# A fixed-point layer in half-batch units, with interval and remainder read from the bits of the shifted value

## The chip, the core and the metric

The kernel runs on one core of a Trainium2 chip. The core has five engines with a queue each: TensorE (PE, matrix products; PEld is its loading of weights), VectorE (DVE), ScalarE (ACT), GpSimd (POOL) and SyncE (SP, which only starts transfers here). Each engine works through its own queue in order; semaphores make an instruction wait for results of other engines. The metric is the device time of one execution in microseconds, lower is better.

## What is computed

The program is a decoder of four layers; each adds an attention, a cross attention and a feed-forward part to the token vectors `x` (8 batches of 256 tokens, 256 features) and normalises after each. The change concerns the very last part, the feed-forward of the fourth layer, a multilayer perceptron in fixed point with a piecewise-linear gelu:

```python
def float2fix(x, bits):                     # round to multiples of 2**-bits
    return round(x * 2**bits) / 2**bits
def pwlin_gelu_basic(x, bits_in, bits_out):
    xq = float2fix(x, bits_in)
    y = interp(xq, _PWL_X, _PWL_Y)          # gelu at 33 points, -4 to 4 in steps of 0.25
    y = where(xq > 4.0, xq, where(xq < -4.0, 0.0, y))
    return float2fix(y, bits_out)
h = einsum('bsd,df->bsf', x, w1) + b1       # 256 -> 1024
h = float2fix(h, 8)
h = pwlin_gelu_basic(h, 8, 8)
h = float2fix(h, 8)
out = einsum('bsf,fd->bsd', h, w2) + b2     # 1024 -> 256
return float2fix(out, 8)
...
x = _layernorm(x + _L3_ffn_ref(x, L3_ffn_w1, L3_ffn_b1, L3_ffn_w2, L3_ffn_b2), axis=-1)
```

In units of 1/256 a hidden value is an integer v; an interval of the gelu is 64 of these units. With n the interval of v (its floor division by 64) and r = v - 64n, the value is `256 gelu(n/4) + 4 (gelu((n+1)/4) - gelu(n/4)) r`, rounded.

## The kernel before

The tokens lie in SBUF twice: `X`, 16 tiles of 128 tokens by 256 features, and `xT`, its transpose, two blocks of 128 features by 2048 tokens. The last parts of the program run batch by batch (256 tokens, two tiles): `l2_ffn` interleaves by hand the expert part of the third layer with `convolve(b)` and `attend(b)`, the two attentions of the fourth layer, for the batch before. After its loop it still has the attentions of batch 7 to issue (`for _ in later: pass`), and then it calls `fixed_point`.

`fixed_point` loops over the 8 batches (`o` in steps of T = 256 tokens). One batch:

- eight blocks of hidden features, two to a PSUM tile `ph`: products with `w1` (L132, each written as two passes in the trace), and one ACT eviction per block with scale 256 and bias (L1594) into `v`, 128 x 2048;
- DVE rounds v by adding and subtracting ROUND = 1.5 x 2^23 (L1596), and finds the interval n in two operations (L1598, L1599);
- ACT takes the gelu at both ends of the interval, `low` (L1601) and `high` (L1603), 128 x 2048 each;
- DVE makes the remainder v - 64n (L1604), the difference high - low (L1605), the product with the remainder (L1606), adds 256 low (L1607) and rounds (L1608);
- for each of the two token tiles PE multiplies v by `w2` (L132, 16 passes) and adds the bias b2 with a product of ones and a row (L134); DVE rounds the result (L1615) and adds the residual (L1616);
- `finish` normalises: statistics on DVE (L163, L164), the inverse root on POOL (L141, L143, since `power` is set for this part), scaling into X on DVE (L187); SP stores each tile to the output.

The pools give `v`, `low`, `high`, `z`, `q` two buffers and `n` one; `ph` and `po` have two PSUM banks each.

The order of the instructions on each engine is not that of the text. When the program is built, a planner with its own estimates of durations takes from all instructions whose operands are ready the one that stands first in the text, engine by engine, and inserts the waits. So the attention of batch 7 comes first where it is ready, and `fixed_point` of the earlier batches fills what is left: on PE, products of its first batch stand at 2508.6 us, before the attention of batch 6 is done at 2551.

Of the kernel before, what the change touches and what calls it, by code (L numbers as in the profile page):

```python
# [11 lines left out]
F32 = mybir.dt.float32  # L12
BF16 = mybir.dt.bfloat16
I32 = mybir.dt.int32
U32 = mybir.dt.uint32
AF = mybir.ActivationFunctionType
ALU = mybir.AluOpType
# [3 lines left out]
P = 128  # L21
B, S, D = 8, 256, 256
NT = B * S // P
NTOK = B * S
# [3 lines left out]
ROUND = 1.5 * 2.0**23  # L28
# [14 lines left out]
class Net:  # L43
# [1241 lines left out]
    def l2_ffn(self, w):  # L1285


        tc = self.tc
        with ExitStack() as ctx:
            w3 = self.load(  # L1290
                ("l3a_win", 2), ("l3a_wout", 2), *((f"l3x_w{n}", 4 if n == "o" else 2) for n in "qkvo"),
                rows=("l3a_bout", "l3a_ln_w", "l3a_ln_b", "l3x_bo"),
            )
            win, wout, wq, wk, wv, wo, bout, ln_w, ln_b, bo = w3
            pool3 = ctx.enter_context(tc.tile_pool(name="a3", bufs=1))
            ps3 = ctx.enter_context(tc.tile_pool(name="a3p", bufs=2, space=PSUM))
            convolve = self.convolution_batches((win, wout, bout, ln_w, ln_b), pool3, ps3)
            attend = self.context_batches((wq, wk, wv, wo, bo), pool3, ps3)
            later = iter(())
            with (  # L1300
                tc.tile_pool(name="f2", bufs=1) as pool,
                tc.tile_pool(name="f2w", bufs=2) as work,
                tc.tile_pool(name="f2p", bufs=2, space=PSUM) as ps,
            ):
                experts = self.expert_batches(w, pool, work, ps)
                for b in range(B):
                    experts(b, later)
                    later = chain(convolve(b), attend(b))
            w4 = self.load(("l3f_w1", 2), ("l3f_w2", 8), rows=("l3f_b2",))
            pool = ctx.enter_context(tc.tile_pool(name="f3", bufs=1))  # L1310
            work = ctx.enter_context(tc.tile_pool(name="f3w", bufs=2))
            ps = ctx.enter_context(tc.tile_pool(name="f3p", bufs=2, space=PSUM))
            for _ in later:
                pass
            self.power = True
            self.fixed_point(w4, pool, work, ps)
# [256 lines left out]
    def fixed_point(self, w, pool, work, ps):  # L1573

        nc = self.nc
        w1, w2, b2_row = w
        FC, T = 8, 256
        ONE = 256.0  # L1580
        b1 = pool.tile([P, FC], F32, name="b1")
        nc.vector.tensor_scalar(b1, self.col("l3f_b1"), ONE, None, ALU.mult)
        b2 = pool.tile([1, D], F32, name="b2")
        nc.vector.tensor_scalar(b2, b2_row, ONE, None, ALU.mult)
        for o in range(0, NTOK, T):
            v = work.tile([P, FC, T], F32, name="v")
            for f in range(0, FC, 2):
                ph = ps.tile([P, 2, T], F32, name="ph")
                for m in range(2):
                    g = f + m  # L1590
                    self.mm(
                        ph[:, m, :], [(w1[:, c, g * P : (g + 1) * P], self.xT[:, c, o : o + T]) for c in range(2)]
                    )
                    nc.scalar.activation(v[:, g, :], ph[:, m, :], AF.Identity, bias=b1[:, g : g + 1], scale=ONE)  # L1594
            v = v.rearrange("p f t -> p (f t)")
            nc.vector.tensor_scalar(v, v, ROUND, ROUND, ALU.add, ALU.subtract)  # L1596
            n = work.tile([P, FC * T], F32, name="n", bufs=1)
            nc.vector.tensor_scalar(n, v, 1 / 64, -31.5 / 64, ALU.mult, ALU.add)  # L1598
            nc.vector.tensor_scalar(n, n, ROUND, ROUND, ALU.add, ALU.subtract)  # L1599
            low = work.tile([P, FC * T], F32, name="low")  # L1600
            nc.scalar.activation(low, n, AF.Gelu, scale=0.25)  # L1601
            high = work.tile([P, FC * T], F32, name="high")
            nc.scalar.activation(high, n, AF.Gelu, bias=self.cst("quarter"), scale=0.25)  # L1603
            nc.vector.scalar_tensor_tensor(v, n, -64.0, v, ALU.mult, ALU.add)  # L1604
            nc.vector.tensor_tensor(high, high, low, ALU.subtract)  # L1605
            nc.vector.scalar_tensor_tensor(v, high, 4.0, v, ALU.mult, ALU.mult)  # L1606
            nc.vector.scalar_tensor_tensor(v, low, ONE, v, ALU.mult, ALU.add)  # L1607
            nc.vector.tensor_scalar(v, v, ROUND, ROUND, ALU.add, ALU.subtract)  # L1608
            h = v.rearrange("p (f t) -> p f t", t=T)
            z = work.tile([P, 2, D], F32, name="z")  # L1610
            for j in range(2):
                po = ps.tile([P, D], F32, name="po")
                self.mm(po, [(h[:, f, j * P : (j + 1) * P], w2[:, f, :]) for f in range(FC)], bias=b2)
                q = work.tile([P, D], F32, name="q")
                nc.vector.tensor_scalar(q, po, ROUND, ROUND, ALU.add, ALU.subtract)  # L1615
                nc.vector.scalar_tensor_tensor(  # L1616
                    z[:, j], q, 1.0 / ONE, self.X[:, o // P + j, :], ALU.mult, ALU.add
                )
            self.finish(o // P, 1, z, self.last)

# [425 lines left out]
```

## Time and profile before

| what | us |
|---|---|
| three runs of the kernel before | 2783.50, 2792.79, 2794.55 |
| their median | 2792.79 |
| the profiled execution, its own time | 2775.67 |
| span of the profiled execution, first to last instruction | 2773.9 |
| first product of `fixed_point` on PE | 2508.6 |
| first L1596 on DVE | 2566.7 |
| last attention operation on DVE (L1565 of batch 7) | 2642.5 |
| last L1608 ends, the last products with `w2` begin | 2754.2 |

The mean TensorE clock granted over the span was 0.873. In a row of the profile "busy" is the time in which an engine had an instruction running; a row of instructions gives engine, operation, output and inputs by the program's names and their count. Lines of the trace can be merged: "x2" is two instructions one after the other. In the rows by stretch each engine's busy time is followed by its number of instructions, then come the granted clock of TensorE, the share of the transfer engines and GB/s. The list of waits reads "who <- whom: total us, times, longest".

### The profile page before, as it was taken

The numbers are of one execution on the slowest core, as the hardware profiler recorded it, in microseconds if no ns is written. First come the engines' busy times: TensorE is split into PE (matmuls) and PEld (weight loads), VectorE is DVE, ScalarE is ACT, GpSimd is POOL, SyncE is SP. The second block draws the span as 40 slices with busy tenths as digits, with TensorE's granted clock in tenths as the row PEclk, the third lists the DMA queues.
The fourth block names the chain that finished last, engine by engine and source line by source line (L and its number), as shares of the span: only waits on it lengthen the run. The fifth ranks groups of instructions, "written<-read, shape, count | busy, mean of one in ns | idle before, by whom it ended". The sixth has DMA issues, their size and how long they took to land.

```text
span 2773.9 us, 40937 instructions
## 1 busy us (share of the span) xinstructions
PE 2171.2 (78%) x14331; PEld 1571.3 (57%) x14331; DVE 1681.6 (61%) x5714; ACT 957.4 (35%) x2197; POOL 891.8 (32%) x949
## 2 busy tenths in 40 slices
PE   8978688699988788438975767887878868777975
PEld 5554588555565467415544345666756656555654
DVE  4654300266667575356767876758668666654876
ACT  2322133234333442104432333343534435433431
POOL 1020121221111124451110136666566565660000
PEclk9988699899998779759997878889989888887987
DMA  2001243200010137420010011111111111120000
GB/s 81 2 1 42 105 149 108 69 7 1 1 62 16 36 106 220 141 80 1 1 42 16 1 65 46 45 43 47 38 41 47 40 43 43 52 73 3 1 20 12
DMA packets 84173, 135.04 MB, mean 49 GB/s; under 512 B 33445, under 2 KB 53045, under 8 KB 82048
## 3 DMA queue, kind: packets, MB, share of 16 engines
q0 software_dynamic: 52288, 79.27, 9.7%
q1 hardware_dynamic: 28924, 49.45, 5.3%
q10 hardware_dynamic: 2756, 3.72, 0.4%
q8 instruction: 114, 1.87, 0.3%
q14 instruction: 91, 0.75, 0.1%
HBM read 242.90 MB, written 17.70 MB: 94 GB/s over the span
## 4 chain that ended last, share of the span: by engine, by line
PE 25%; DVE 16%; issue 6%; ACT 3%; another core or an unknown queue 2%; POOL 2%; DMA 0%; ACTq 0%; POOLq 0%; DVEq 0%
PE po L1401 5%; PE pp L132 4%; PE s L132 4%; PE po L132 3%; DVE junk L1349 2%; DVE low L478 1%; PE ph L132 1%; PE s L1547 1%; PE sc L132 1%; PE s L1525 1%; POOL rows L893 1%; PE po L1382 1%; PE sc L445 1%; DVE X L187 1%
## 5 line engine op out<-in xcount | busy, mean ns | idle before, releaser
L893 POOL DMA_INDIRECT rows<-in_l2f_table_dram,index x512 | 530.5, 1036 | 348.8 <-issue 110.7
L1401 PE MATMUL po<-rows,diag 128*128 128x256 f32 x768 | 231.2, 437 | 90.7 <-ACT diag L1400 54.4
L1349 DVE SCALAR_TENSOR_TENSOR junk<-rows,X 128x256 f32<-128x256 f32 x512 | 214.9, 420 | 53.6 <-DMA rows<-in_l2f_table_dram,index 28.4
L1401 PEld LDWEIGHTS po<-rows,diag 128*128 128x128 f32 x768 | 153.0, 213 | 142.8 <-ACT diag L1400 67.2
L132 PE MATMUL pp<-xT,w 128*128 128x256 f32 (+1 forms) x672 | 196.9, 435 | 35.1 <-issue 20.4
L132 PE MATMUL ph<-xeT,we 128*128 128x128 f32 x1248 | 183.7, 291 | 20.9 <-DMA we<-in_l0f_experts_dram,wrow 16.5
L132 PEld LDWEIGHTS ph<-xeT,we 128*128 128x128 f32 x1248 | 170.1, 201 | 41.7 <-DMA we<-in_l0f_experts_dram,wrow 17.9
L553 POOL TENSOR_TENSOR aT<-sides,inv 128x256 f32<-128x256 f32 x64 | 46.8, 731 | 441.6 <-DVE sides L551 275.3
L132 PEld LDWEIGHTS pp<-xT,w 128*128 128x128 f32 x672 | 141.6, 218 | 69.2 <-issue 29.7
L1400 ACT ACTIVATE diag<-ident,dots 128x128 f32<-128x128 f32 x384 | 134.1, 394 | 129.9 <-PE po L1401 58.8
L173 PE MATMUL pt<-ident,X 128*128 128x128 f32 x352 | 76.3, 330 | 117.6 <-DVE X L187 68.9
L174 ACT COPY xT<-pt 128x512 f32<-128x512 f32 x88 | 51.6, 587 | 328.1 <-PE pt L173 229.7
L893 POOL DMA_INDIRECT xe<-xd,take x87 | 85.2, 979 | 208.0 <-PE pt L908 81.6
L141 POOL TENSOR_SCALAR rs_v<-ln_mv 128x2 f32<-128x2 f32 x48 | 12.5, 260 | 389.8 <-DVE ln_mv L164 362.1
L173 PEld LDWEIGHTS pt<-ident,X 128*128 128x128 f32 x352 | 49.4, 163 | 152.7 <-issue 73.0
L132 PE MATMUL py<-we,hT 128*128 128x256 f32 x496 | 129.8, 386 | 0.9 <-DVE hT L1037 0.9
L1014 DVE TENSOR_TENSOR y<-py,we 128x256 f32<-128x256 f32 x23 | 9.8, 425 | 199.0 <-PE py L132 199.0
L517 ACT ACTIVATE e<-sc 128x512 f32<-128x512 f32 (+1 forms) x155 | 82.0, 602 | 107.2 <-PE sc L445 93.5
L1008 ACT ACTIVATE hT<-ph,we 128x128 f32<-128x128 f32 x184 | 65.5, 367 | 121.0 <-PE ph L132 91.3
L187 DVE TENSOR_SCALAR X<-z,ln_mv,rs_y 128x256 f32<-128x256 f32 x192 | 73.3, 424 | 54.3 <-POOL rs_y L143 52.4
L445 PE MATMUL sc<-kv,qv 32*128 32x128 f32 (+2 forms) x1448 | 99.8, 315 | 2.5 <-DVE sides L551 1.0
L445 PE MATMUL sc<-qv,kv 32*128 32x128 f32 (+2 forms) x1396 | 99.1, 347 | 0.0
(492 smaller groups left out, 5205.2 us busy)
## 6 DMA issues: line engine op xcount, KB each, us to landing
we<-in_l1f_experts_dram SPq DMA_DIRECT2D x32, 384.0 KB
yd<-y SPq DMA_DIRECT2D x32, 256.0 KB
rows<-in_l2f_table_dram,index POOLq DMA_INDIRECT x512
w<-in_l2x_w_dram SPq DMA_DIRECT2D x1, 4096.0 KB
yd<-y SPq DMA_DIRECT2D x23, 128.0 KB
X<-in_x_dram SPq DMA_DIRECT2D x8, 256.0 KB
xd<-X ACTq DMA_DIRECT2D x8, 256.0 KB
xd<-X SPq DMA_DIRECT2D x8, 256.0 KB
```

The source lines that it names most:

```text
L132: self.nc.tensor.matmul(out, lhsT=lhsT, rhs=rhs, start=n == 0, stop=n == last and bias is None)
L173: nc.tensor.transpose(pt[:, c, j, :], self.X[:, i0 + j * step, c * P : (c + 1) * P], self.ident)
L174: nc.scalar.copy(self.xT4[:, :, i0 : i0 + step + 1 : step, :], pt)
L187: nc.vector.tensor_scalar(self.X[:, i, :], z[:, j, :], mv[:, j, 0:1], r[:, j : j + 1], ALU.subtract, ALU.mult)
L445: nc.tensor.matmul(sc[: shape[0], part], lhsT=lhsT, rhs=rhs, start=mask is None, stop=True, skip_group_check=True)
L517: lambda r, sc: nc.scalar.activation(e0[m][:n0, r], sc, AF.Exp),
L553: nc.gpsimd.tensor_tensor(out, split(both), split(inv), ALU.mult)
L893: self.nc.gpsimd.indirect_dma_start(out=out, out_offset=None, in_=table, in_offset=bass.IndirectOffsetOnAxis(ap=index, axis=0), **({} if r ...
L1008: nc.scalar.activation(hT[:, g + f, :], ph[:, f, :], AF.Gelu, bias=b1[:, g + f : g + f + 1])
L1349: nc.vector.scalar_tensor_tensor(junk, row, 1.0, self.X[:, i, :], ALU.mult, ALU.mult, accum_out=out)
L1400: nc.scalar.activation(diag, self.ident, AF.Copy, scale=dots[:, k : k + 1])
L1401: nc.tensor.matmul(po, lhsT=diag, rhs=rows[:, k, D:], start=False, stop=g + k == H * K - 2)
```

## The change

A unit is now half of a batch's hidden features (four blocks, 128 x 1024), 16 units in all, and a loop issues for each u the steps `first(u + 2)`, `gelu(u + 1)`, `between(u)` and `second(u)`. `first` adds ROUND on ACT and leaves it in: the low bits of the float are then the integer v. `gelu` shifts these bits right by six and flips the exponent bits, which makes the float 2^23 + 2^16 + n, in one DVE operation; the gelus take the offset off again by their bias (a column of `shift`). A second DVE operation keeps the low six bits and sets an exponent so that the float is 2^25 + 4r. The difference of the gelus is formed by GpSimd. `between` has three DVE operations: remainder times difference, plus 256 low, rounding. `second` runs for every second unit: the products of both token tiles go into one PSUM bank, b2 is added by DVE from a tile that was spread over the partitions once at the start, and rounding and residual take both tiles at once. `v`, `n`, `q`, `z` have two buffers of half or double width, `low` and `high` three, `f` four.

```diff
@@ l2_ffn @@
-            work = ctx.enter_context(tc.tile_pool(name="f3w", bufs=2))
+            work = ctx.enter_context(tc.tile_pool(name="f3w", bufs=3))
@@ fixed_point @@
-        FC, T = 8, 256
+        FC, T, H = 8, 256, 4
...
-        b2 = pool.tile([1, D], F32, name="b2")
-        nc.vector.tensor_scalar(b2, b2_row, ONE, None, ALU.mult)
-        for o in range(0, NTOK, T):
-            v = work.tile([P, FC, T], F32, name="v")
...
-            v = v.rearrange("p f t -> p (f t)")
-            nc.vector.tensor_scalar(v, v, ROUND, ROUND, ALU.add, ALU.subtract)
-            n = work.tile([P, FC * T], F32, name="n", bufs=1)
-            nc.vector.tensor_scalar(n, v, 1 / 64, -31.5 / 64, ALU.mult, ALU.add)
-            nc.vector.tensor_scalar(n, n, ROUND, ROUND, ALU.add, ALU.subtract)
-            low = work.tile([P, FC * T], F32, name="low")
-            nc.scalar.activation(low, n, AF.Gelu, scale=0.25)
-            high = work.tile([P, FC * T], F32, name="high")
-            nc.scalar.activation(high, n, AF.Gelu, bias=self.cst("quarter"), scale=0.25)
-            nc.vector.scalar_tensor_tensor(v, n, -64.0, v, ALU.mult, ALU.add)
-            nc.vector.tensor_tensor(high, high, low, ALU.subtract)
-            nc.vector.scalar_tensor_tensor(v, high, 4.0, v, ALU.mult, ALU.mult)
-            nc.vector.scalar_tensor_tensor(v, low, ONE, v, ALU.mult, ALU.add)
-            nc.vector.tensor_scalar(v, v, ROUND, ROUND, ALU.add, ALU.subtract)
...
+        b2 = pool.tile([P, D], F32, name="b2")
+        pp = ps.tile([P, 2, T], F32, name="ph")
+        nc.tensor.matmul(pp[:, 0, :], lhsT=self.ones, rhs=b2_row, start=True, stop=True)
+        nc.scalar.mul(b2, pp[:, 0, :], ONE)
+        shift = pool.tile([P, 3], F32, name="shift")
+        for n, value in enumerate((ROUND, -0.25 * (2.0**23 + 2.0**16), -0.25 * (2.0**23 + 2.0**16 - 1.0))):
+            nc.gpsimd.memset(shift[:, n : n + 1], value)
+        units = [(o, h) for o in range(0, NTOK, T) for h in range(0, FC, H)]
+        vs, fs, gelus = {}, {}, {}
+
+        def first(u):
+            o, h = units[u]
+            v = vs[u] = work.tile([P, H, T], F32, name="v", bufs=2)
...
+                    nc.scalar.activation(v[:, f + m, :], ph[:, m, :], AF.Identity, bias=b1[:, g : g + 1], scale=ONE)
+            nc.scalar.activation(v, v, AF.Identity, bias=shift[:, 0:1])
+
+        def gelu(u):
+            v = vs.pop(u).rearrange("p f t -> p (f t)").bitcast(I32)
+            n = work.tile([P, H * T], F32, name="n", bufs=2)
+            nc.vector.tensor_scalar(
+                n.bitcast(I32), v, 6, 0x4B000000 ^ 0x4B000000 >> 6, ALU.arith_shift_right, ALU.bitwise_xor
+            )
+            low = work.tile([P, H * T], F32, name="low")
+            nc.scalar.activation(low, n, AF.Gelu, bias=shift[:, 1:2], scale=0.25)
+            high = work.tile([P, H * T], F32, name="high")
+            nc.scalar.activation(high, n, AF.Gelu, bias=shift[:, 2:3], scale=0.25)
+            f = fs[u] = work.tile([P, H * T], F32, name="f", bufs=4)
+            nc.vector.tensor_scalar(f.bitcast(I32), v, 63, 0x4C000000, ALU.bitwise_and, ALU.bitwise_or)
+            nc.gpsimd.tensor_tensor(high, high, low, ALU.subtract)
+            gelus[u] = low, high
+
+        def between(u):
+            low, rise = gelus.pop(u)
+            f = fs[u]
+            nc.vector.scalar_tensor_tensor(f, f, 2.0**25, rise, ALU.subtract, ALU.mult)
+            nc.vector.scalar_tensor_tensor(f, low, ONE, f, ALU.mult, ALU.add)
+            nc.vector.tensor_scalar(f, f, ROUND, ROUND, ALU.add, ALU.subtract)
+
+        def second(u):
+            o, h = units[u]
+            if h == 0:
+                return
...
             for j in range(2):
-                po = ps.tile([P, D], F32, name="po")
-                self.mm(po, [(h[:, f, j * P : (j + 1) * P], w2[:, f, :]) for f in range(FC)], bias=b2)
...
+                self.mm(
+                    po[:, j, :], [(fb[f // H][:, f % H, j * P : (j + 1) * P], w2[:, f, :]) for f in range(FC)]
                 )
+            q = work.tile([P, 2, D], F32, name="q", bufs=2)
+            nc.vector.tensor_tensor(q, po, b2.unsqueeze(1).to_broadcast([P, 2, D]), ALU.add)
+            nc.vector.tensor_scalar(q, q, ROUND, ROUND, ALU.add, ALU.subtract)
...
+        count = len(units)
+        for u in range(-2, count):
+            if u + 2 < count:
+                first(u + 2)
+            if 0 <= u + 1 < count:
+                gelu(u + 1)
+            if u >= 0:
+                between(u)
+                second(u)
```

More of the change, by code (lines that the diff above doesn't have):

```diff
@@ L1582, in fixed_point @@
         nc.vector.tensor_scalar(b1, self.col("l3f_b1"), ONE, None, ALU.mult)
-        b2 = pool.tile([1, D], F32, name="b2")
-        nc.vector.tensor_scalar(b2, b2_row, ONE, None, ALU.mult)
-        for o in range(0, NTOK, T):
-            v = work.tile([P, FC, T], F32, name="v")
-            for f in range(0, FC, 2):
+        b2 = pool.tile([P, D], F32, name="b2")
[10 more added lines that the diff above has]
+            v = vs[u] = work.tile([P, H, T], F32, name="v", bufs=2)
+            for f in range(0, H, 2):
                 ph = ps.tile([P, 2, T], F32, name="ph")
                 for m in range(2):
-                    g = f + m
+                    g = h + f + m
                     self.mm(
@@ L1593, in fixed_point @@
                     )
-                    nc.scalar.activation(v[:, g, :], ph[:, m, :], AF.Identity, bias=b1[:, g : g + 1], scale=ONE)
-            v = v.rearrange("p f t -> p (f t)")
-            nc.vector.tensor_scalar(v, v, ROUND, ROUND, ALU.add, ALU.subtract)
-            n = work.tile([P, FC * T], F32, name="n", bufs=1)
-            nc.vector.tensor_scalar(n, v, 1 / 64, -31.5 / 64, ALU.mult, ALU.add)
-            nc.vector.tensor_scalar(n, n, ROUND, ROUND, ALU.add, ALU.subtract)
-            low = work.tile([P, FC * T], F32, name="low")
@@ L1608, in fixed_point @@
-            nc.vector.tensor_scalar(v, v, ROUND, ROUND, ALU.add, ALU.subtract)
-            h = v.rearrange("p (f t) -> p f t", t=T)
-            z = work.tile([P, 2, D], F32, name="z")
-            for j in range(2):
-                po = ps.tile([P, D], F32, name="po")
-                self.mm(po, [(h[:, f, j * P : (j + 1) * P], w2[:, f, :]) for f in range(FC)], bias=b2)
[L1614 to L1617, printed above, removed]
-                )
@@ new lines, in between @@
+        def between(u):
[8 more added lines that the diff above has]
+                return
+            fb = [fs.pop(n).rearrange("p (f t) -> p f t", t=T) for n in (u - 1, u)]
+            po = ps.tile([P, 2, D], F32, name="po")
+            for j in range(2):
+                self.mm(
+                    po[:, j, :], [(fb[f // H][:, f % H, j * P : (j + 1) * P], w2[:, f, :]) for f in range(FC)]
+                )
+            q = work.tile([P, 2, D], F32, name="q", bufs=2)
+            nc.vector.tensor_tensor(q, po, b2.unsqueeze(1).to_broadcast([P, 2, D]), ALU.add)
+            nc.vector.tensor_scalar(q, q, ROUND, ROUND, ALU.add, ALU.subtract)
+            z = work.tile([P, 2, D], F32, name="z", bufs=2)
+            nc.vector.scalar_tensor_tensor(z, q, 1.0 / ONE, self.X[:, o // P : o // P + 2, :], ALU.mult, ALU.add)
+            self.finish(o // P, 1, z, self.last)
```

## The prediction

> **What bounds the kernel now.** First the page's head; then, since the changed function is the program's last stage, the busy table by stretch from 2551 us (the attention of token batch 6 ends there) to the end; then the chain of waits and the wait list there; last, two places where GpSimd and VectorE met.
>
> ```profile
> span 2773.9 us, 40937 instructions
> ...
> PE 2171.2 (78%) x14331; PEld 1571.3 (57%) x14331; DVE 1681.6 (61%) x5714; ACT 957.4 (35%) x2197; POOL 891.8 (32%) x949
> ```
>
> ```profile
> 2551.00:2577.00 26.00, 24.13 (x101) 17.95 (x102) 17.11 (x42) 16.41 (x28) 0.00 (x0) 0.88 0.00 0
> 2577.00:2620.00 43.00, 37.38 (x164) 28.71 (x163) 42.88 (x55) 15.93 (x22) 0.00 (x0) 0.92 0.00 1
> 2620.00:2647.00 27.00, 25.93 (x151) 21.09 (x149) 12.29 (x43) 11.79 (x30) 2.02 (x4) 1.00 0.00 1
> 2647.00:2691.00 44.00, 30.51 (x123) 23.15 (x124) 35.88 (x45) 14.34 (x17) 2.80 (x4) 0.84 0.07 24
> 2691.00:2735.00 44.00, 36.16 (x142) 28.18 (x141) 33.16 (x34) 16.43 (x24) 1.85 (x4) 0.88 0.04 12
> 2735.00:2774.00 39.00, 13.21 (x47) 9.34 (x45) 19.49 (x24) 4.28 (x3) 2.79 (x4) 0.71 0.04 13
> ```
>
> Columns after the length: PE, PEld, DVE, ACT, POOL busy, then the granted clock. DVE is full at first (42.88 of 43 us), PE is full while the attention of batch 7 runs, and from 2647 on neither is.
>
> ```profile
> 2745.98 2.30 DVE high L1605
> 2748.30 2.30 DVE v L1606
> 2750.63 2.30 DVE v L1607
> 2752.95 1.24 DVE v L1608
> 2754.24 5.76 PE po L132 x16
> ```
>
> ```profile
> PE po L132 <- DVE v L1608: 35.1, 4, 16.7
> ...
> ACT low L1601 <- DVE n L1599: 31.7, 6, 9.8
> ```
>
> The chain is that of the last batch: DVE alone from 2745.98, then PE, whose first 16 passes take 5.76 us (3.72 at full clock). PE waited 35.1 us in all for the last rounding, and the gelus 31.7 us for the interval, since whole batches go through DVE, ACT, DVE and PE in turn. L1605 starts at 2658.65, 2702.24 and 2745.98 for every second batch: 43.7 us for two, 21.8 us a batch.
>
> ```profile
> 1549.82 2.50 POOL L1815 TENSOR_TENSOR z<-X,b 128x512 f32<-128x512 f32 x2 [29.68 <-ACT b L1797]
> ...
> 1549.80 1.37 DVE L1790 SCALAR_TENSOR_TENSOR top<-top,cat_sc,bias 128x64 f32<-128x64 f32 x1
> 1551.21 1.17 DVE L1791 TENSOR_SCALAR top<-top 128x64 f32<-128x64 f32 x1
> ...
> 2650.87 1.16 POOL L141 TENSOR_SCALAR rs_v<-ln_mv 128x2 f32<-128x2 f32 x1 [3.96 <-DVE ln_mv L164]
> ...
> 2650.73 1.23 DVE L1598 TENSOR_SCALAR n<-v 128x2048 f32<-128x2048 f32 x1
> ```
>
> Two DVE operations on 64 columns took 1.37 and 1.17 us, each until a GpSimd addition was over; a GpSimd operation on two columns took 1.16 us (0.22 elsewhere), until DVE's L1598 was over. They exclude each other.
>
> **The Trainium skill.** "SBUF — State Buffer", Who interferes with whom: VectorE in a two-port mode, or with two SBUF inputs, and a reading GpSimd share a port pair as an exclusive lock; the second to start waits for the whole of the first. The lines above agree. "GPSIMD Engine Reference", Performance versus the Vector engine: an elementwise two-input operation is about twice as long on GpSimd (4497 against 2293 ns at 2048 columns). The trace agrees: L575, 128x512, takes 1.27 us there, and L1469, the same shape, 0.68 on DVE. "ScalarE: Activation LUTs", What ACT_TABLE_LOAD costs: a load takes 1283 ns, as each row ACT_TABLE_LOAD here shows.
>
> **The change, part by part.** Durations of new widths lie between measured ones: tensor_scalar, 0.42 at 512 (L1657) and 1.22 at 2048 (L1596), so 0.69 us at 1024; two SBUF inputs, 0.42 at 256 (L1616) and 2.29 at 2048, so 1.22; GpSimd tensor_tensor, 0.73 at 256 (L553) and 1.27 at 512, so 2.35; ACT with a bias column, 0.475 at 256 (L1594) and 1.99 at 2048 (L1603), so 1.13.
>
> 1. DVE, per batch, before: 4 x 2.29 + 4 x 1.22 = 14.0; q and z 4 x 0.42 = 1.7; norm 2 x (0.42 + 0.17 + 0.41) = 2.0 (L163, L164, L187); 17.7 us. After: per unit 3 x 0.69 + 2 x 1.22 = 4.5, twice 9.0; q from PSUM 0.69 (as L1463), its rounding 0.42, z 0.69; norm 2.0; 12.8 us. Over 8 batches 142 becomes 103, 39 us less. That the integer operations take both ports at 1024 columns isn't shown (L1243, int32, has only 32): 0.69 if they do, 1.22 if not, which adds 17 us in all; a gain is excluded, as it is one pass either way. I take 0.69, since the row is a plain tensor_scalar of four-byte type.
> 2. POOL gets 16 subtractions of 2.35 = 37.5 us, beside 8 x 0.93 = 7.4 of the norm's L141 and L143, which now queue behind them; only L187, which writes the output tile, waits for those. The new wait is DVE's, in the first operation of `between`, for the subtraction of one unit earlier; behind it on DVE stand the integer operations of the next unit, and the gelus on ACT wait for these, so a late subtraction delays a whole unit. Lower bound: hidden, 0; upper: the whole 37.5 taken from DVE by the port. Not taken by the port are the norm statistics and q (1.9 a batch). I let half of these lie beside POOL.
> 3. ACT: per batch 8 x 0.475 + 1.91 + 1.99 = 7.7 before, 8 x 0.475 + 6 x 1.13 = 10.6 after, with the shift by ROUND. 23 us more, off the path as 79 us were busy of 223; its cover is that idle time, and without it (gelus next to the end of a unit) half of it, 12 us, would show. Smaller gelus between attention's Exp and Silu may add table loads: 0 to 6 at 1.28 us; I put them into the misfit below.
> 4. PE loses the 16 bias products, 0.62 us each in the chain: 9.9 us. One product that spreads b2, one ACT and three memsets at the start lie beside attention: 0. No DMA is added or moved.
> 5. v is free once both integer operations have read it, and f has four buffers; before, v was held until po had read it, and three evictions (L1594) waited 8.4 us for that.
> 6. The first unit needs four evictions (2561.06 in the trace) instead of eight, so DVE starts about 5 us sooner; the last round of 16 us before po becomes one of 0.69 + 2.26 + 2.35 + 3.13 = 8.4.
>
> **The sum.** From 2551 the DVE was busy for 160.8 us, 19 of them attention. After: 103 + 19 = 122, plus POOL 45, less 8 side by side: 159 us for the shared port. PE from 2551, at 3.72 us for 16 passes at clock 1.00: 504 passes of this layer 117 us, the attention's 62 wide ones 14 and its short ones some 18: 150. So the port leads narrowly. At 93% filled (between 42.88/43 in one stretch and 69/88 in the two from 2647; my choice) 159 becomes 171. Add 9 us of idle DVE in the first stretch, and the end: 13.5 us from the last rounding: 19.7 before, less 2.4 for 8 of 32 passes that can run earlier, 1.2 for two bias products, and 2.6 of q, z and norm that the 159 already hold. 2551 + 171 + 9 + 13.5 = 2744.5, so 29 us less than the span of 2773.9. Around the span lie 1.8 us (the profiled execution took 2775.7). Against the median of the runs, 2792.8, the same difference gives 2763 us. The profiled execution was 17 us under that median, so the difference is what I predict.
>
> **Rivals.**
> - *Port as bound* (the forecast), 2763: for it, the measured exclusion; against it, that DVE gives the port up whenever it waits for PE. Chance 0.54; own range 2748 to 2778.
> - *PE as bound*, the subtractions fall into DVE's gaps: 150/0.93 = 161, 2 at the start, 5 of the last unit's round laid bare, 11 after po: 2730, 44 less, 2749. For it: 25.93 of 27 us at 2620. Chance 0.18.
> - *Orders of the queues don't interlock*: on ACT the gelus stand behind evictions that wait for ph, ph behind po. Then a batch goes round as po 7.44, ph 3.72, eviction and shift 1.6, gelus 2.26, subtraction 2.35, DVE 3.13, six hand-overs 0.6: 21.1 us. Five batches from 2647 gain 3.5, the end some 5: 2784. For it: L1594 waited 46.2 us for ph. Against it: at 2660.86 L1596 of the next batch stood between L1605 and L1606, so orders do interleave. Chance 0.18.
> - *Slower: the subtraction stands alone.* DVE's back-to-back operations keep the port, the subtraction gets it when DVE has run dry, and units don't overlap: 0.69 + 2.26 + 2.35 + 3.13 + 0.4 = 8.8 a unit, with po laid bare 17.7 + 7.4 = 25.1 us a batch. Five batches lose 16.5: 2809. It decides once a round passes 21.8 us. Against it: at 2650.87 the waiting GpSimd got the port at the end of one DVE operation. Chance 0.10.
>
> **Numbers.** Half a per cent, 14 us, is about what can be told from no change. Faster by more: all of the second, nearly all of the first, a tenth of the third: 0.73; within: the rest of these, 0.17; slower 0.10. Range 2733 to 2792: it takes in the PE case with some 15 us more of fill, and the third, with the 17 us of the integer operations at one pass; it leaves out the slower case and the far ends.
>
> **What would show it.** L1605's successor on POOL at 2.35 us where DVE is still, longer where it had to wait; DVE's 1024-column operations with two inputs showing durations well over 1.22 wherever a subtraction runs; integer operations at 0.69; a distance of 17 to 18 us between batches after attention; PE's wait for the last rounding well below 35 us. Wrong: integer operations at 1.22, distances of 21 us or more, gelu table loads in a row, or POOL and DVE side by side at full speed, which would put PE first.

## The result, and the profile after

The changed kernel takes 2765.84 us (median of five runs, 2757.05 to 2771.54) against 2792.79: a ratio of 0.991, 95% interval 0.9883 to 0.9937, 27 us less. The profiled execution took 2765.84 us.

Line numbers of the changed kernel: L1606 eviction of `ph`, L1607 shift by ROUND; L1612 interval, L1616 and L1618 the two gelus, L1620 remainder, L1621 subtraction on POOL; L1627 to L1629 the three operations of `between`; L1642, L1643, L1645 q, its rounding, z.

The page's head, and the busy table by stretch from the end of the attention of batch 6, which here lies at 2566 us:

```profile
span 2764.1 us, 40977 instructions
...
PE 2166.8 (78%) x14292; PEld 1569.7 (57%) x14301; DVE 1651.2 (60%) x5721; ACT 984.6 (36%) x2236; POOL 928.0 (34%) x968
```

```profile
2566.00:2592.00 26.00, 15.98 (x58) 12.12 (x58) 10.43 (x28) 19.45 (x30) 2.34 (x1) 0.76 0.00 0
2592.00:2640.00 48.00, 44.20 (x195) 33.79 (x196) 36.25 (x73) 26.73 (x42) 9.49 (x4) 0.88 0.00 1
2640.00:2667.00 27.00, 23.83 (x129) 19.82 (x127) 19.24 (x42) 18.03 (x29) 6.00 (x5) 1.00 0.00 1
2667.00:2705.00 38.00, 34.02 (x147) 28.05 (x148) 30.48 (x49) 21.22 (x30) 13.01 (x10) 0.96 0.08 28
2705.00:2740.00 35.00, 28.83 (x131) 23.86 (x129) 24.11 (x40) 20.99 (x30) 11.96 (x8) 1.00 0.05 16
2740.00:2764.00 24.00, 10.92 (x32) 8.23 (x32) 9.98 (x22) 0.17 (x1) 4.20 (x5) 0.64 0.07 22
sum 198.00, PE 157.77 PEld 125.88 DVE 130.50 ACT 106.59 POOL 47.00; mean PE 26.30 PEld 20.98 DVE 21.75 ACT 17.76 POOL 7.83
```

The span is only 9.8 us shorter than before (2773.9), but the stage is 25 us shorter: from the same instruction, the scaling that ends the attention of batch 6 (L187, 2550.46 before, 2565.87 now), to the end it was 223.4 us and is 198.2. The 15 us come from unchanged code ahead of the stage; a second profile of the kernel before, further down, has them too. So from here on a stage time is used that doesn't depend on what came earlier: from the start of the last operation of the experts on DVE (L1404 of the unchanged code) to the end of the span. It is 265.8 us before and 241.3 after.

DVE looks unfilled: 24.11 of 35 us even at the end. The wait list of that stretch (2566 to 2764) and the timeline say what it does in between:

```profile
DVE f L1627 <- POOL high L1621: 23.7, 9, 4.7
...
ACT low L1616 <- DVE n L1612: 14.7, 7, 3.4
...
PE po L132 <- DVE f L1629: 10.1, 4, 4.3
```

```profile
2690.26 2.35 POOL L1621 TENSOR_TENSOR high<-high,low 128x1024 f32<-128x1024 f32 x1 [4.22 <-ACT high L1618]
2690.28 0.68 DVE L1642 TENSOR_TENSOR q<-po,b 128x512 f32<-128x512 f32 x1
...
2691.00 1.90 DVE L1643 TENSOR_SCALAR q<-q 128x512 f32<-128x512 f32 x1
...
2692.82 1.21 DVE L1627 SCALAR_TENSOR_TENSOR f<-f,high 128x1024 f32<-128x1024 f32 x1
...
2699.82 2.39 POOL L1621 TENSOR_TENSOR high<-high,low 128x1024 f32<-128x1024 f32 x1 [1.19 <-ACT high L1618]
...
2702.24 1.22 DVE L1627 SCALAR_TENSOR_TENSOR f<-f,high 128x1024 f32<-128x1024 f32 x1 [2.25 <-POOL high L1621]
2703.39 0.68 DVE L1612 TENSOR_SCALAR n<-v 128x1024 int32<-128x1024 int32 x1
...
2704.16 1.15 ACT L1616 ACTIVATE low<-n,shift 128x1024 f32<-128x1024 f32 x1 [2.89 <-DVE n L1612]
```

Twice DVE does nothing useful while POOL subtracts. At 2691.00 the rounding L1643, elsewhere 0.42 us, is recorded with 1.90, until the subtraction ends at 2692.61: held at the port. q (L1642), with one input in PSUM, ran freely beside it. At 2702.24 DVE had waited 2.25 us for the data. Behind L1627 stands the interval L1612 of the next unit, and the gelu L1616 waits for that: a loop DVE, ACT, ACT, POOL, DVE, which the chain of waits follows from 2680 to the last unit (at 2691.00 through the held L1643). The subtractions start at 2683.68, 2690.26, 2699.82, 2706.43, 2716.76 and 2723.34: 16.1 to 16.9 us for two units, a batch.

So two readings fit. Either the port is what is short (as predicted), or the loop's latency is, and a better order would hide the subtraction. The experiments had to tell these apart, and both from TensorE as the bound.

### The profile page after: what moved, and what is told of

Same layout as the page of the kernel before. It is cut to its first block, busy times and chain, and to the rows that moved or that the text cites. A ratio compares the mean times of both kernels' runs of the same rounds, so it can differ in the third digit from the quotient of the medians.

```text
span 2764.1 us, 40977 instructions
## 1 busy us (share of the span) xinstructions
PE 2166.8 (78%) x14292; PEld 1569.7 (57%) x14301; DVE 1651.2 (60%) x5721; ACT 984.6 (36%) x2236; POOL 928.0 (34%) x968
## 4 chain that ended last, share of the span: by engine, by line
PE 35%; DVE 23%; issue 9%; POOL 4%; ACT 4%; DMA 4%; another core or an unknown queue 4%; POOLq 0%; ACTq 0%; DVEq 0%
PE po L1401 5%; PE s L132 4%; PE pp L132 4%; PE sc L132 4%; DVE low L478 3%; PE ph L132 2%; DMA xe<-xd,take 2%; PE sc L445 2%; DVE low L462 2%; PE pt L132 2%; POOL rows L893 1%; PE sc L566 1%; DVE X L187 1%; DVE junk L1349 1%
## 5 line engine op out<-in xcount | busy, mean ns | idle before, releaser
L1401 PE MATMUL po<-rows,diag 128*128 128x256 f32 x768 | 237.9, 447 | 106.1 <-ACT diag L1400 57.6
L132 PE MATMUL pp<-xT,w 128*128 128x256 f32 (+1 forms) x672 | 195.0, 432 | 31.2 <-issue 15.6
L187 DVE TENSOR_SCALAR X<-z,ln_mv,rs_y 128x256 f32<-128x256 f32 x192 | 72.0, 417 | 55.9 <-POOL rs_y L143 51.8
L893 POOL DMA_INDIRECT yg<-yd,slot x80 | 77.2, 965 | 67.2 <-issue 31.9
```

The source lines that it names most:

```text
L132: self.nc.tensor.matmul(out, lhsT=lhsT, rhs=rhs, start=n == 0, stop=n == last and bias is None)
L187: nc.vector.tensor_scalar(self.X[:, i, :], z[:, j, :], mv[:, j, 0:1], r[:, j : j + 1], ALU.subtract, ALU.mult)
L893: self.nc.gpsimd.indirect_dma_start(out=out, out_offset=None, in_=table, in_offset=bass.IndirectOffsetOnAxis(ap=index, axis=0), **({} if r ...
L1401: nc.tensor.matmul(po, lhsT=diag, rhs=rows[:, k, D:], start=False, stop=g + k == H * K - 2)
```

## The experiments

All were timed in five rounds beside the kernel before on the same chip, save the second profile of the kernel before itself. The chips differ (median before 2648.7, 2651.7 and 2792.8 us in the three groups), so ratios are compared. A stage time comes from one profile. It hardly depends on the chip: what a kernel gains by its stage time agrees with what it gains by its ratio to within 4 us, and two profiles of one kernel differed by 0.9 and 1.5 us.

| kernel | subtraction by | ratio to before, 95% interval | stage, us |
|---|---|---|---|
| before | DVE | 1 | 265.8 (again: 264.3) |
| changed | POOL | 0.991 (0.9883 to 0.9937); again 0.9912 | 241.3 (again: 240.4) |
| e4 units, old arithmetic | DVE | 0.9888 (0.9866 to 0.9911) | 235.0 |
| f2 new arithmetic, whole batches | DVE | 0.988 (0.986 to 0.99) | 235.0 |
| e1 changed, subtraction on DVE | DVE | 0.9834 (0.9813 to 0.9855) | 223.9 |
| f3 as e1, b2 on PE | DVE | 0.9855 (0.9831 to 0.9879) | 228.5 |
| e3 changed, no subtraction | none | 0.9812 (0.979 to 0.9833) | 220.0 |
| f1 as e3, subtraction nobody reads | POOL | 0.9925 (0.9902 to 0.9949) | 247.8 |
| g1 as e3, memsets on POOL | none | 0.984 (0.9807 to 0.9874) | 223.9 |
| e2 one unit further ahead | POOL | 0.9905 (0.9884 to 0.9927) | 242.1 |
| f4 interval put first | POOL | 0.9916 (0.9897 to 0.9935) | 244.7 |

**e1: the subtraction on DVE.**

```diff
-            nc.gpsimd.tensor_tensor(high, high, low, ALU.subtract)
...
         def between(u):
             low, rise = gelus.pop(u)
             f = fs[u]
+            nc.vector.tensor_tensor(rise, rise, low, ALU.subtract)
```

> The changed kernel with the subtraction of the gelus as the first VectorE operation of `between` instead of GpSimd's. Shared port as bound: 159 us of port work lose 37.5 of GpSimd and gain 16 x 1.22 = 19.5 of VectorE, so about 13 us off the changed kernel (some 40 below before, ratio 0.986). Loop through GpSimd as bound (VectorE stands at `between` for the subtraction, with the next unit's interval operation behind it): the 2.36 us and its two hand-overs leave the loop, VectorE needs 15.2 us a batch instead of the 16.95 measured, 8 to 12 us off the changed kernel (0.987), and VectorE's first operation of `between` waits for almost nothing. TensorE as bound: no change from the changed kernel (0.991).

The stage is 17.4 us shorter than with POOL, and the ratio's interval lies below that of the changed kernel. This is the fastest kernel here that computes everything, and it does more on DVE: 16 x 1.22 us. Groups of e1's stage (busy, mean ns, then idle time before them):

```profile
L1627 DVE SCALAR_TENSOR_TENSOR f<-f,high 128x1024 f32<-128x1024 f32 x16 | 19.5, 1216 | 0.0
L1626 DVE TENSOR_TENSOR high<-high,low 128x1024 f32<-128x1024 f32 x16 | 19.5, 1221 | 6.6 <-ACT high L1618 6.6
```

The subtraction waited 6.6 us for the gelus; the product after it waited for nothing. Port and loop had both foretold a gain (13 us and 8 to 12, less than came), so e1 doesn't decide between them; it only excludes TensorE as the bound of the changed kernel.

**e3: no subtraction at all**, the line of POOL taken out and nothing put in its place.

> The changed kernel with the subtraction left out (the upper gelu is used in the place of the difference). This is the whole cost of the subtraction. Shared port: 159 falls to 122, under TensorE's 150, so the layer ends where TensorE lets it: 10 to 17 us off the changed kernel (0.985 to 0.987). Loop through GpSimd: the same size, 10 to 15 us, by distances of 14.5 to 15.5 us a batch. TensorE as bound of the changed kernel already: no more than 3 us off (0.990).

The stage falls by 21.3 us. That is more than the 10 to 17 us that the port's case had foretold. So the subtractions cost 21.3 us on POOL, and 3.9 on DVE (e1 against e3, by one profile each; the ratios' intervals overlap).

**e2 and f4: the loop loosened.** e2 issues the gelus one unit earlier in the text:

```diff
-        for u in range(-2, count):
-            if u + 2 < count:
-                first(u + 2)
-            if 0 <= u + 1 < count:
-                gelu(u + 1)
+        for u in range(-3, count):
+            if u + 3 < count:
+                first(u + 3)
+            if 0 <= u + 2 < count:
+                gelu(u + 2)
```

with five buffers for `f` and one for `q` and `z`.

> The changed kernel with the gelus of a unit issued one unit earlier (two units ahead of `between`), same work on every engine. Shared port as bound: the same time as the changed kernel (ratio 0.991), distances of 17 us a batch. Loop through GpSimd as bound: the subtraction has a whole unit of time, VectorE's wait for it (23.7 us in the changed kernel) falls below 5 us, distances of 15 to 15.5 us a batch, 8 us off the changed kernel (0.988). TensorE as bound: the same as the changed kernel, with the wait moved to another place.

The time is that of the changed kernel, but so is the order: in e2's trace L1612 again comes right after an L1627 that has waited (25.7 us in all); why the planner kept it isn't shown. So e2 didn't do what it was meant to, and decides nothing. f4 forces the order by a false dependence, one more DVE operation a unit on one column (2.2 us in all); `ns` holds the tiles `n`:

```diff
         def between(u):
             low, rise = gelus.pop(u)
             f = fs[u]
+            if u + 1 < count:
+                nc.vector.scalar_tensor_tensor(f[:, 0:1], ns[u + 1][:, 0:1], 0.0, f[:, 0:1], ALU.mult, ALU.add)
```

> The changed kernel, subtraction on GpSimd, with one VectorE operation on one column ahead of `between` (it adds 0 times the next unit's interval to the remainder) that makes the planner put the interval operation of unit u + 1 ahead of `between` of unit u, which it had not done. The port is asked for just as much. Shared port as bound: same as the changed kernel (0.991), distances of 17 us. Loop through GpSimd as bound: gelus and subtraction of unit u + 1 run beside `between` of unit u, VectorE's wait for the subtraction falls below 8 us, distances of 15 to 15.5 us, ratio 0.985 to 0.988.

Here the order changed and the wait went, but the time didn't. The groups of f4's stage, and its timeline (L1631 to L1633 are `between`, L1623 the subtraction):

```profile
L1633 DVE TENSOR_SCALAR f<-f 128x1024 f32<-128x1024 f32 x16 | 29.1, 1817 | 0.3
...
L1632 DVE SCALAR_TENSOR_TENSOR f<-low,f 128x1024 f32<-128x1024 f32 x16 | 23.9, 1494 | 0.3
L1631 DVE SCALAR_TENSOR_TENSOR f<-f,high 128x1024 f32<-128x1024 f32 x16 | 19.6, 1224 | 0.8
```

```profile
2565.27 1.23 DVE L1632 SCALAR_TENSOR_TENSOR f<-low,f 128x1024 f32<-128x1024 f32 x1
2565.60 3.11 POOL L1623 TENSOR_TENSOR high<-high,low 128x1024 f32<-128x1024 f32 x1 [3.52 <-ACT high L1620]
2566.53 2.72 DVE L1633 TENSOR_SCALAR f<-f 128x1024 f32<-128x1024 f32 x1
...
2569.17 0.68 DVE L1646 TENSOR_TENSOR q<-po,b 128x512 f32<-128x512 f32 x1
```

L1631 had 0.8 us of idle time ahead of it, instead of 23.7. But the rounding L1633 takes 1.82 us in the mean instead of 0.69 and L1632 1.49 instead of 1.22: 16 x (1.13 + 0.27) = 22 us. What was a wait for the data has become a wait at the port, of the same size. Read the pair: the subtraction begins while L1632 runs and takes 3.11 us instead of 2.36, as it must wait for L1632; then L1633 waits for the subtraction. The distance between batches was 17.8 us, against 16.9 in the changed kernel. So to take the loop's wait away gains nothing: the port then takes as much.

**f1: the same subtraction, but nobody waits for it.** To e3 is added, with one buffer instead of two for `q` and `z` to make room:

```diff
+            spare = work.tile([P, H * T], F32, name="spare", bufs=1)
+            nc.gpsimd.tensor_tensor(spare, high, low, ALU.subtract)
```

> The kernel without the subtraction (e3, ratio 0.9812), with 16 GpSimd subtractions of 128x1024 added whose result goes to a spare tile that nobody reads: VectorE takes the upper gelu as it is and never waits for GpSimd, but the shared port is asked for as in the changed kernel (q and z with one buffer, to make room). Shared port as the price of the subtraction: VectorE's operations are held up by up to 37.5 us and the time goes back to the changed kernel's, 0.989 to 0.991. Loop through GpSimd as the price: the time stays at e3's, 0.981 to 0.984.

27.8 us of stage come back, though DVE never waits for a result of these subtractions. It is more than the 21.3 that they cost in the changed kernel: here 13 of the 16 begin while DVE runs an operation with two inputs and wait for it first, so that they take 50.7 us in all instead of 37.8. The single buffers explain little of it: g1, below, has them too, and its stage is only 3.9 us above e3's. In f1's groups (L1622 is the subtraction, L1629 the second operation of `between`, which takes 1.22 us in e3):

```profile
L1629 DVE SCALAR_TENSOR_TENSOR f<-low,f 128x1024 f32<-128x1024 f32 x16 | 33.7, 2109 | 0.2
...
L1628 DVE SCALAR_TENSOR_TENSOR f<-f,high 128x1024 f32<-128x1024 f32 x16 | 19.5, 1220 | 13.0 <-ACT high L1618 13.0
...
L1612 DVE TENSOR_SCALAR n<-v 128x1024 int32<-128x1024 int32 x16 | 15.1, 944 | 4.3 <-ACT v L1607 4.3
```

DVE's row L1629 grew by 14.2 us, L1612 by 4.1. Both forms of operation are held, with one input and with two.

**g1: POOL busy without reading.** As f1, with three memsets in the place of a subtraction, paced by a one-column DVE operation, and the same single buffers.

```diff
+            nc.vector.scalar_tensor_tensor(f[:, 0:1], spare[:, 0:1], 0.0, f[:, 0:1], ALU.mult, ALU.add)
+            for _ in range(3):
+                nc.gpsimd.memset(spare, 0.0)
```

> As f1 (no subtraction for VectorE, GpSimd busy with work that nobody waits for), but GpSimd's work of a unit is three memsets of the 128x1024 spare tile, about 2.75 us, which write and read nothing, paced by a one-column VectorE operation ahead of `between`. If it is reads of SBUF that keep VectorE's two-input operations out: those stay at 1.22 us, only the one-input operations of 1024 columns are stretched where they meet a memset, and the time lies near e3's, 0.981 to 0.986. If any GpSimd work of that length holds VectorE up (or the planner's order with more instructions does): as f1, 0.990 to 0.993.

```profile
L1630 POOL MEMSET spare<- 128x1024 f32 x48 | 48.2, 1005 | 83.0 <-DVE f L1628 81.2
...
L1631 DVE SCALAR_TENSOR_TENSOR f<-f,high 128x1024 f32<-128x1024 f32 x16 | 19.5, 1221 | 11.0 <-ACT high L1620 11.0
L1632 DVE SCALAR_TENSOR_TENSOR f<-low,f 128x1024 f32<-128x1024 f32 x16 | 19.5, 1219 | 0.2
...
L1614 DVE TENSOR_SCALAR n<-v 128x1024 int32<-128x1024 int32 x16 | 12.9, 807 | 4.3 <-ACT v L1609 4.3
L1622 DVE TENSOR_SCALAR f<-v 128x1024 int32<-128x1024 int32 x16 | 11.7, 732 | 0.0
```

48.2 us of memsets cost 3.9 us of stage (the 16 pacing operations alone keep DVE busy for 2.4), where 50.7 us of subtraction cost 27.8. DVE's operations with two SBUF inputs keep their 1.22 us beside a memset; one-input operations are stretched where they meet one, L1614 from 0.69 to 0.81 in the mean, L1622 from 0.69 to 0.73. It isn't work on POOL as such that holds DVE's two-input operations, but POOL's reading of SBUF; a one-input operation of this width can be held by a writing POOL as well. How much the latter would cost if memsets met more of these operations wasn't tried.

**e4 and f2: each half of the change alone.** e4 keeps the units, and b2 on DVE, and takes the old arithmetic, all on DVE:

```diff
-            nc.scalar.activation(v, v, AF.Identity, bias=shift[:, 0:1])
...
+            nc.vector.tensor_scalar(v, v, ROUND, ROUND, ALU.add, ALU.subtract)
+            nc.vector.tensor_scalar(n, v, 1 / 64, -31.5 / 64, ALU.mult, ALU.add)
+            nc.vector.tensor_scalar(n, n, ROUND, ROUND, ALU.add, ALU.subtract)
...
+            nc.vector.scalar_tensor_tensor(f, n, -64.0, v, ALU.mult, ALU.add)
...
+            nc.vector.tensor_tensor(rise, rise, low, ALU.subtract)
+            nc.vector.scalar_tensor_tensor(f, rise, 4.0, f, ALU.mult, ALU.mult)
```

> Units, order and b2 by VectorE as in the changed kernel, but the old arithmetic, all of it on VectorE (three rounding passes and four two-input operations a unit, no shift on ScalarE, no GpSimd). Pipelining brings the gain: VectorE has 142 + 19 us to do and is filled to 93 per cent, so 20 to 28 us below before (ratio 0.990 to 0.993), about the time of the changed kernel. The relief of VectorE brings the gain: no more than 8 us below before (0.997 or above).

f2 keeps the whole batches of the kernel before and takes the new arithmetic, with the subtraction on DVE:

```diff
-            nc.vector.tensor_scalar(v, v, ROUND, ROUND, ALU.add, ALU.subtract)
+            nc.scalar.activation(v, v, AF.Identity, bias=shift[:, 0:1])
...
-            nc.vector.tensor_scalar(n, v, 1 / 64, -31.5 / 64, ALU.mult, ALU.add)
-            nc.vector.tensor_scalar(n, n, ROUND, ROUND, ALU.add, ALU.subtract)
+            nc.vector.tensor_scalar(
+                n.bitcast(I32), bits, 6, 0x4B000000 ^ 0x4B000000 >> 6, ALU.arith_shift_right, ALU.bitwise_xor
+            )
...
-            nc.vector.scalar_tensor_tensor(v, n, -64.0, v, ALU.mult, ALU.add)
+            nc.vector.tensor_scalar(bits, bits, 63, 0x4C000000, ALU.bitwise_and, ALU.bitwise_or)
```

> The kernel before with the new arithmetic alone: whole batches in the old order, shift by ROUND on ScalarE, interval and remainder from the bits, subtraction on VectorE, b2 on TensorE. VectorE has 10.5 us a batch for this arithmetic instead of 14.0, ScalarE 1.99 more. If the arithmetic is worth what it takes off VectorE: 28 us less work, 15 to 25 us below before (0.991 to 0.994). If the chain of a batch counts, where 1.99 us of ScalarE replace 3.5 of VectorE: 8 to 12 us (0.996). If it is worth nothing without units: 0.998 or above.

Either alone takes about 31 us off the stage, by the ratios at least as much as the whole change; both together, without POOL, 42. Both gained more than was expected of them (e4 20 to 28 us, f2 15 to 25). In f2 batches follow each other in 15.1 to 16.0 us instead of 21.8, which is more than the 3.5 us of work that a batch lost on DVE, so the order became better too. Why the planner's order fits better there wasn't tried.

**f3: b2 on TensorE again**, in e1, with q rounded straight from PSUM.

```diff
-                    po[:, j, :], [(fb[f // H][:, f % H, j * P : (j + 1) * P], w2[:, f, :]) for f in range(FC)]
+                    po[:, j, :], [(fb[f // H][:, f % H, j * P : (j + 1) * P], w2[:, f, :]) for f in range(FC)], bias=b2
...
-            nc.vector.tensor_tensor(q, po, b2.unsqueeze(1).to_broadcast([P, 2, D]), ALU.add)
-            nc.vector.tensor_scalar(q, q, ROUND, ROUND, ALU.add, ALU.subtract)
+            nc.vector.tensor_scalar(q, po, ROUND, ROUND, ALU.add, ALU.subtract)
```

> The kernel with the subtraction on VectorE (e1, ratio 0.9834), with b2 added by 16 products on TensorE again, and q rounded straight from PSUM in one operation instead of two. TensorE as bound: 9.9 us more (0.987). VectorE as bound: 8 x 0.42 = 3.4 us less (0.982). Neither: within 0.001 of e1.

The ratios' intervals overlap; the stage of the one profiled execution is 4.6 us longer. With TensorE's 9.9 us more and DVE's 3.4 less, that would be a stage in which both count; from one trace this is an indication and no more.

**The two kernels again**, unchanged, on the chip of g1.

> The changed kernel itself on the chip of these runs: 0.988 to 0.994 if its ratio does not depend on the chip, with distances of 17 us a batch, and the trace for comparison with e1, e3, f1 and f4.

> The kernel before itself, one look, for its trace on the chip of these runs: distances of 43 to 44 us for two batches from the end of the attention, as in the trace shown, if this stage does not depend on the chip.

The ratio of the changed kernel came out the same. The trace of the kernel before had its stage in 264.3 us, and L1605 came 43.6 to 44.9 us after its run of two batches earlier, as in the first trace; its last L1565 lies 15.2 us later and its span, 2789.0, is 15.1 longer. So the 15 us ahead of the stage come with no change of code.

## Why the prediction was right

The forecast of 2763 us came from a difference of 29 us; the medians differ by 27, and the stage by 25. Its mechanism, the port that VectorE and GpSimd share, held up in f1, f4 and g1 as a cost that no order removed. But in the changed kernel itself most of that cost shows as waits for a result, which the forecast had counted as time at the port (step 2), and the sum came out close in part because terms too small and a term too large made up for each other (step 6). By its steps:

1. *DVE.* The integer operations take 0.69 us, the upper bound of 1.22 is out. DVE is busy for 130.5 us in the stage. Of these 11.1 are not work but holding at the port, by comparing its rows with the same rows of e1 (L1629, L1645, L1643) and of the kernel before (the rest): L1629 1.5, L1645 2.0, L1643 1.4, and operations on two columns (L146, L151, L154) 6.2. The work is 119.4 us, forecast 122.
2. *POOL.* 16 subtractions, 37.8 us, as forecast; 18.9 of them lie within waits of L1627 (the other 4.8 us of its waits came before the subtraction had begun), 11.1 show as holding, and the remaining 8 lie beside DVE's work or its other idle time, as reckoned. DVE's work, these two, and 5.9 us of waits of L187 for the norm's POOL operations make 119.4 + 18.9 + 11.1 + 5.9 = 155.3 us, against 159 forecast for the port. That the size fits is in part luck: in 18.9 of these us DVE waited for data, not for the port, and only f4 shows that the port takes about as much once that wait is gone. That "a late subtraction delays a whole unit" was right as a description of the loop, but it is no extra cost on top of the port's.
3. *ACT* has 27.4 us more, forecast 23 and up to six table loads. There are six more (ten instead of four), 7.7 us, so the work itself grew by 19.7. Four of the six come at the start, where gelus and the attention's functions take turns:

```profile
2580.17 1.28 ACT L1616 ACT_TABLE_LOAD   x1
...
2581.47 1.15 ACT L1616 ACTIVATE low<-n,shift 128x1024 f32<-128x1024 f32 x1
2582.63 1.28 ACT L1452 ACT_TABLE_LOAD   x1
...
2585.88 1.28 ACT L1618 ACT_TABLE_LOAD   x1
2587.17 1.15 ACT L1618 ACTIVATE high<-n,shift 128x1024 f32<-128x1024 f32 x1
2588.34 1.28 ACT L1452 ACT_TABLE_LOAD   x1
2588.40 2.34 POOL L1621 TENSOR_TENSOR high<-high,low 128x1024 f32<-128x1024 f32 x1 [65.39 <-ACT high L1618]
```

The duration of 1.28 us is that of "ScalarE: Activation LUTs", What ACT_TABLE_LOAD costs, in the Trainium skill. Here three loads lie between the first interval operation and the first subtraction, though the forecast had put loads into the misfit.

4. *PE* lost 9.5 us (167.3 to 157.8), forecast 9.9. Its worth on the path seems less (4.6 us in f3's stage, not resolved by the runs).
5. *v freed earlier.* The evictions' wait for ph fell from 46.2 us to 19.6; this part wasn't isolated.
6. *Start and end.* The start is the term that was mis-sized: 9 us of idle DVE were forecast for the first stretch, and it is 15.6 of 26. DVE's first operation of the layer on `v` comes 3.8 us sooner, not 5 (12.4 us after the scaling that ends the attention of batch 6 instead of 16.2), and the first L1627 then stands until 2590.78 behind the loads above. This 6.6 us is more than the 4.7 by which the stage missed its 193.5. From the last rounding to the end it is 17.5 us instead of 19.7; less the 2.6 of q, z and norm that the port's sum holds, 14.9 against 13.5 forecast. What is left of the stage, 198.2 - 15.6 - 14.9 = 167.7 us, is 3.3 less than the 171 that the forecast had made of the port's 159 with a filling of 93%, a number it had chosen.

The pace of 16.1 to 16.9 us a batch from 2684 on lies just under the 17 to 18 forecast. But the rivals weren't wholly beside the point. As in the slower one, units hardly overlap on DVE: 6.6 and 10.3 us for the two of a batch, 8.5 a unit against its 8.8. It would have decided only if the products with `w2` had been laid bare as well, and these run beside the next units. TensorE as bound is out: e1 does the same PE work in 17 us less.

What the prediction didn't ask is whether the third part of the change should be there. Its upper bound for the subtraction, 37.5 us taken from DVE, was in the sum; a subtraction on DVE would have been 19.5 us by the same rows. The sum contained the better kernel.

## What to carry to other kernels

Before an elementwise operation that reads SBUF goes from VectorE to GpSimd, price it as time taken from VectorE: most of its GpSimd duration can go, as a wait for the result or as holding of VectorE's two-input and two-port operations. Here 2.36 us on GpSimd replaced 1.22 on VectorE; the 37.8 us of subtractions cost 21.3 us of stage, on VectorE 3.9, and the change kept 25 of the 42 us that units and new arithmetic were worth. The Trainium skill warns of it in "Perfetto Trace Analysis", Optimizing Scalar/DVE Operations: moving operations between these two engines might not help; here it cost 17.4 us of stage. And a wait that disappears from one row should be looked for in the durations of its neighbours before it is called gone.

## What the runs showed of the hardware

- For VectorE's two-input operations the exclusion goes by what GpSimd reads: beside memsets they kept 1.22 us, beside subtractions the second operation of `between` was held to 2.1 in the mean (g1, f1). The Trainium skill says so in "SBUF — State Buffer", Who interferes with whom, where an operation with two SBUF inputs is said to contend with a GpSimd instruction that reads and not with one that only writes; these runs agree.
- Either side waits for the other: the subtraction took 2.36 us alone and 3.36 in the mean of the 13 that began during a two-input operation of VectorE (f1).
- A VectorE operation with one of its two inputs in PSUM ran beside a subtraction at its own 0.68 us (L1642 at 2690.28 in the changed kernel).
- The time at the port is within an instruction's recorded duration, so a held VectorE counts as busy: 11.1 of 130.5 us in the changed kernel.
